# A post-norm layer on one core: short contractions filled up to 128 rows, and two sums of Wo on another engine

## The chip, the core and the metric

The kernel runs on one core of a Trainium2 chip. A core has five engines that run their own instruction streams and wait for one another through semaphores: TensorE (PE in the profile; its weight loads are listed apart as PEld), VectorE (DVE), ScalarE (ACT), GpSimd (POOL), and SyncE (SP), which here only issues DMAs. The metric is the device time of one execution in microseconds. All arithmetic is in 32-bit floats; each matmul of the program appears in the trace as two PE instructions, each transpose on PE as one.

## The reference

One layer: attention with rotary positions and a causal mask, then a layer norm, then a dense layer with a routed low-rank addition, then a layer norm.

```python
x = layernorm(x + attention(x, Wq, bq, Wk, bk, Wv, bv, Wo, bo))
x = layernorm(x + ffn(x, ...))

def ffn(x, W_base, b_base, lora_A, lora_B, router_W, router_b, domain_prior, active):
    y = einsum('bth,oh->bto', x, W_base) + b_base
    z = einsum('bth,erh->bter', x, lora_A[active])
    contribs = einsum('bter,eor->bteo', z, lora_B[active]) * 2.0
    logits = (einsum('bth,eh->bte', x, router_W) + router_b)[..., active]
    alpha = softmax(log(domain_prior[active] + 1e-12) + logits)
    return y + einsum('bteo,bte->bto', contribs, alpha)
```

x is (2, 512, 512): 2 sequences of 512 tokens with 512 features. There are 32 query heads and 8 key heads of 128; 4 of 16 experts are active, each with 8 low-rank rows, so A has 32 rows (EAR) and the router 4 (EA).

## The kernel before

The attention is worked in 16 units (a key head and a sequence each). A unit has 16 slots; a slot is one block of 32 tokens by 4 query heads, 128 rows of scores. The function `slot(T)` writes out by hand, for every slot T, what each engine is given: on PE a score matmul, pieces of the next unit's query projection, of the key and value projections, of the output projection of an earlier unit, and the product of the probabilities with v; on DVE the masked maximum of slot T-1, the reciprocals of T-2, the 32x32 transposes of T-4, the rotations of q and k and the adds into x_sb; on ACT the exponentials and the copies. The score has two PSUM banks, so a score needs the exponential of two slots earlier to be done. Engines work strictly in the order written. Work that isn't tied to each slot is put at a slot with `put(T, f)` and is given out at that slot's end.

The projections use a scheme of seven instead of eight block products, which needs sums and differences of blocks beforehand. For the output projection these are the four of `wo_sums` (L621): step 0 makes t1 = b12 - b11, step 1 makes t2 = b22 - t1, step 2 overwrites b12 with b22 - b12, step 3 makes t4 = b21 - t2, each over 128x512 elements. `wo_products` (L638) reads t2 in its step 2 and t1 in its step 3, two and three slots after the set of weights comes in, b12 in step 4 and t4 in step 6. A set serves both sequences of a key head, except for the last two key heads, which are worked one sequence at a time ("single"). For the single sets the four sums stand on POOL, one slot before the set comes in (L930); only two single sets take this path, since the last two sets use the plain product `wo_mm`. POOL also makes the sums of the context (`ctx_sums`, L633), of Wq (`w_sums`, L426), and the last addition of each rotation (L376).

In the setup, the rows of A and of the router are gathered into ar_act (36 partitions) and transposed on PE into arT (L284, tile ta); B is transposed into the first 32 rows of bmT, whose row 32 is the bias b_base (33 partitions); the prior, replicated over 128 columns in lp_rep (4 partitions), is spread over the partitions by a product with the identity (L312, tile pl).

After the attention each of the 8 token tiles is an object `Ffn`. `base` multiplies the normed tile with W_base, A and the router (L767); `logits` and `alphas` make the weighted factor zs on DVE and ACT; `low_rank` transposes it on PE (L803, tile tz) and copies it on DVE into the first 32 rows of zT, whose row 32 is ones (L743, 33 partitions); `finish` (L808) adds zT times bmT, two matmuls of 256 columns; `add` adds the residual and starts the second norm's statistics (L814, L693). The last tile, fc, takes its base product in two halves with the same low-rank product at their end (L829), and `route` (L771) for A and the router. The order of these calls is written out by hand at the end of the kernel (L1089 to L1203), partly between the last slots.

Of the kernel before, what the change touches and what calls it, by code (L numbers as in the profile page):

```python
# [9 lines left out]
F32 = mybir.dt.float32  # L10
I32 = mybir.dt.int32
AF = mybir.ActivationFunctionType
ALU = mybir.AluOpType
AX = mybir.AxisListType

P = 128
# [13 lines left out]
def postln_layer_kernel(  # L30
# [33 lines left out]
    nc = tc.nc  # L64
    B, S, HID = x.shape
# [4 lines left out]
    O = W_base.shape[0]  # L70
    OC = O // P
    EA = active.shape[0]
    EAR = EA * RK
# [19 lines left out]
    def set_of(u):  # L93
        return u // B if u < MIXED else MIXED // B + u - MIXED

    def set_units(n):
        return [u for u in range(NU) if set_of(u) == n]
# [4 lines left out]
    const = ctx.enter_context(tc.tile_pool(name="const", bufs=1))  # L102
# [18 lines left out]
    OH, ARH = O // 2, EAR // 2  # L121
    WX_COLS = OH + ARH + EA
    arT = const.tile([P, KC, EAR + EA], F32, name="arT")
    bmT = const.tile([EAR + 1, O], F32, name="bmT")
    lp_bc = const.tile([P, EA], F32, name="lp_bc")
    ident = const.tile([P, P], F32, name="ident")
    maskw = const.tile([P, S], F32, name="maskw")
# [14 lines left out]
    setup = setup_stack.enter_context(tc.tile_pool(name="setup", bufs=1))  # L142
# [41 lines left out]
    for r in range(QB):  # L184
        nc.gpsimd.tensor_copy(maskw[ts(r, BLK), S - BLK :], tri[ts(r, BLK), r, :])
    nc.gpsimd.memset(eps_sb, LN_EPS)
    for z in zt:
        nc.gpsimd.memset(z, 0.0)

# [28 lines left out]
    nc.gpsimd.dma_start(out=act_p, in_=active.partition_broadcast(P))  # L218
    lane = setup.tile([P, 1], I32, name="lane")
    nc.gpsimd.iota(lane, pattern=[[0, 1]], base=0, channel_multiplier=1)  # L220
    ar_act = setup.tile([EAR + EA, HID], F32, name="ar_act")
    rb_act = setup.tile([EA, 1], F32, name="rb_act")
    pr_act = setup.tile([EA, 1], F32, name="pr_act")
    b_act = setup.tile([P, EA, BJ * RK], F32, name="b_act")
# [1 line left out]
    idx = {}  # L226
# [31 lines left out]
    def gather(dst, src, rows):  # L258
        nc.gpsimd.indirect_dma_start(
            out=dst, out_offset=None, in_=src,  # L260
            in_offset=bass.IndirectOffsetOnAxis(ap=rows, axis=0),
        )

    def gather_experts():
        gather(ar_act[:EAR, :], lora_A.rearrange("e r n -> (e r) n"), idx["a"])
        gather(ar_act[EAR:, :], router_W, idx["e"])
        for a in range(EA):
            gather(b_act[:, a, :], lora_B.rearrange("e (p j) r -> (e p) (j r)", j=BJ), idx["b"][:, a : a + 1])

# [10 lines left out]
    def lora_weights(step):  # L280
        if step == 0:
            ta = ps_wo.tile([P, KC, EAR + EA], F32, tag="wx", name="ta")
            for c in range(KC):
                nc.tensor.transpose(ta[:, c, :], ar_act[:, ts(c, P)], ident[: EAR + EA, : EAR + EA])  # L284
            nc.vector.tensor_copy(arT, ta)
            nc.vector.tensor_copy(b_jar, b_act.rearrange("p a (j r) -> p j a r", r=RK))
        else:

            tbm = ps_wo.tile([EAR, BJ, P], F32, tag="wx", name="tbm")
            for j in range(BJ):  # L290
                nc.tensor.transpose(tbm[:, j, :], b_jar[:, j, :, :].rearrange("p a r -> p (a r)"), ident)
            nc.vector.tensor_copy(bmT[:EAR, :].rearrange("k (p j) -> k j p", j=BJ), tbm)

    pr = {}

    def prior_weights(step):

        if step == 0:
            pr_eps = setup.tile([EA, 1], F32, name="pr_eps")
            nc.vector.tensor_scalar(pr_eps, pr_act, PRIOR_EPS, None, ALU.add)  # L300
            pr["lp"] = setup.tile([EA, 1], F32, name="lp")
            nc.scalar.activation(pr["lp"], pr_eps, AF.Ln)
        elif step == 1:
            lpb = setup.tile([EA, 1], F32, name="lpb")
            nc.vector.tensor_tensor(lpb, pr["lp"], rb_act, ALU.add)
            ones = setup.tile([EA, P], F32, name="ones")
            nc.vector.memset(ones, 1.0)
            pr["rep"] = setup.tile([EA, P], F32, name="lp_rep")
            nc.vector.tensor_scalar(pr["rep"], ones, lpb, None, ALU.mult)
        else:  # L310
            pl = ps_wo.tile([P, EA], F32, tag="wx", name="pl")
            nc.tensor.matmul(pl, lhsT=pr["rep"], rhs=ident[:EA, :EA], start=True, stop=True)  # L312
            nc.vector.tensor_copy(lp_bc, pl)


# [302 lines left out]
    def wo_block(n, c_half, n_half):  # L618
        return wos[n][:, CH * c_half : CH * (c_half + 1), ts(n_half, NHALF)]

    def wo_sums(n, step, engine=nc.vector):  # L621

        if step == 0:
            wt[n] = wow.tile([P, 3, CH, NHALF], F32, tag="wt", name=f"wt_{n}", bufs=1)
        t1, t2, t4 = (wt[n][:, m] for m in range(3))
        b11, b12, b21, b22 = (wo_block(n, c_half, n_half) for c_half in range(2) for n_half in range(2))
        engine.tensor_tensor(
            *((t1, b12, b11), (t2, b22, t1), (b12, b22, b12), (t4, b21, t2))[step], ALU.subtract)
# [54 lines left out]
    class Norm:  # L683


        def __init__(self, pool, n, name):
            self.mv = pool.tile([P, n, 2], F32, name=f"mv_{name}")
            self.rstd = pool.tile([P, n], F32, name=f"rstd_{name}")
            self.pool = pool
# [43 lines left out]
    class Ffn:  # L733
# [3 lines left out]
        def __init__(self, t, banks, norm1, norm2, i):  # L737
            self.t, self.banks, self.norm1, self.norm2, self.i = t, banks, norm1, norm2, i
            self.x = x_sb[:, t, :]
            self.xT = ffn_pool.tile([P, KC, P], F32, name=f"x1T_{t}")  # L740
            self.y = ffn_pool.tile([P, O], F32, name=f"y_{t}")

            self.zT = ffn_pool.tile([EAR + 1, P], F32, name=f"zT_{t}")  # L743
            nc.gpsimd.memset(self.zT[EAR:, :], 1.0)

        def own(self, shape, name):
            return ffn_pool.tile(shape, F32, name=f"{name}_{self.t}")
# [113 lines left out]
    def put(slot, f):  # L861
        extra.setdefault(slot, []).append(f)
# [3 lines left out]
    def v_tile(gg, t, pool, tag):  # L866
        for c in range(KC):
            v_mm(gg, t, c, pool, tag)

    put(T_BEGIN, gather_experts)  # L870
    for n, gg, t in [(2 * t - 1, 0, TPB + t) for t in range(TPB)] + [(2 * t + 11, 1, t) for t in range(TPB)]:
        put(n, lambda gg=gg, t=t: v_tile(gg, t, ps_wo, "wx"))
# [4 lines left out]
    for k in range(3):  # L877
        put(-4 + k, lambda k=k: prior_weights(k))
        if k < 2:
            put(12 + 4 * k, lambda k=k: lora_weights(k))  # L880
# [41 lines left out]
    def wo_from(u):  # L922
        return UNIT * u + LAG_WO
# [3 lines left out]
    for n in range(NSETS - 2):  # L927
        single = len(set_units(n)) == 1
        for k in range(4):
            put(wo_from(set_units(n)[0]) + (-1 if single else (0, 1, 1, 3)[k]),  # L930
                lambda n=n, k=k, engine=nc.gpsimd if single else nc.vector: wo_sums(n, k, engine))


    weigh_at = {}
# [137 lines left out]
    ffn_pool = ctx.enter_context(tc.tile_pool(name="ffn", bufs=1))  # L1072
# [181 lines left out]
```

## Time and profile before

| | us |
|---|---|
| median of 3 runs (lowest to highest) | 826.52 (826.05 to 826.85) |
| the profiled execution | 826.17 |
| its span, first to last instruction | 824.2 |
| PE busy in the span | 814.9 |
| DVE busy | 598.2 |
| POOL busy | 327.8 |
| PE granted clock | 0.999 |

The profiled execution took 1.97 us more than its span; what is worked out from the trace is a difference of spans. Lines of the profile name an engine, a line of the kernel, the operation, the tiles written and read, the partitions and elements, and the count; times are in microseconds from the start of the span. A matmul's form such as 33*128 33x256 is weights of 33 rows and 128 columns and moving data of 33 rows and 256 columns. Matmuls overlap, so durations of neighbours add up to more than the time between their starts.

### The profile page before, as it was taken

The page shows a single profiled execution, that of the slowest core. Times are in us where ns is not written, and L with a number is a line of the kernel's source. Part 1 is how long each engine was busy: PE and PEld are TensorE (multiplying, and loading weights), DVE is VectorE, ACT ScalarE, POOL GpSimd, SP SyncE. Part 2 cuts the span into 40 slices and gives each one's busy share as a digit, 9 for nine tenths or more (in the row PEclk, how much of TensorE's full clock was granted, in tenths as well). Part 3 has the DMA queues.
Part 4 walks back from the last instruction along what each step waited for, and adds up shares of the span by engine and source line. Part 5 has one row for each costly group of instructions (what it writes and reads, how often), then busy time and mean ns, then how long its engine had stood idle before and what let it go on. Part 6 is the DMA issues. An engine that isn't in the chain of part 4 may idle for free.

```text
span 824.2 us, 11178 instructions
## 1 busy us (share of the span) xinstructions
PE 814.9 (99%) x3381; PEld 596.9 (72%) x3381; DVE 598.2 (73%) x1964; ACT 379.0 (46%) x1058; POOL 327.8 (40%) x374
## 2 busy tenths in 40 slices
PE   9999999999999999999999999999999999999997
PEld 5567777777777778777777878777777777655565
DVE  5368877687879886787867786787867678973445
ACT  1236453553545454545535454445535454563254
POOL 6464343511534445322443245353445626410032
PEclk9999999999999999999999999999999999999999
DMA  9015627445465636364554536365544636474211
GB/s 293 34 50 150 203 73 194 126 121 160 117 177 137 183 90 206 89 159 148 149 146 115 179 90 205 91 187 170 137 136 121 195 84 202 138 254 142 77 38 64
DMA packets 84414, 115.99 MB, mean 141 GB/s; under 512 B 6525, under 2 KB 64237, under 8 KB 82306
## 3 DMA queue, kind: packets, MB, share of 16 engines
q1 hardware_dynamic: 83682, 114.98, 48.3%
q8 instruction: 27, 0.44, 0.2%
q0 software_dynamic: 448, 0.14, 0.2%
q14 instruction: 33, 0.27, 0.1%
q10 hardware_dynamic: 224, 0.16, 0.1%
HBM read 71.21 MB, written 44.04 MB: 140 GB/s over the span
## 4 chain that ended last, share of the span: by engine, by line
PE 94%; DVE 2%; POOL 2%; DMA 1%; ACT 0%; issue 0%; SPq 0%; DVEq 0%; POOLq 0%
PE pc L602 16%; PE sc L546 14%; PE qx L434 11%; PE wx L434 11%; PE qy L434 9%; PE wy L434 8%; PE pp L355 5%; PE kx L434 4%; PE vx L512 4%; PE py L767 3%; PE po L674 3%; PE pv L338 3%; PE tp L275 1%; PE py L808 1%; DMA pT<-db 1%; DMA db<-zt 0%
## 5 line engine op out<-in xcount | busy, mean ns | idle before, releaser
L554 DVE CUSTOM_DVE_ANT_0 sc<-sc,maskw 128x288 f32<-128x288 f32 (+15 forms) x256 | 114.2, 446 | 146.3 <-PE sc L546 144.7
L561 ACT ACTIVATE p<-sc,nmax 128x288 f32<-128x288 f32 (+15 forms) x256 | 124.3, 485 | 202.8 <-DVE nmax L554 180.4
L602 PE MATMUL pc<-pT,v 128*128 128x512 f32 x320 | 165.5, 599 | 0.1
L546 PE MATMUL sc<-kT,qT 128*128 128x160 f32 (+15 forms) x512 | 162.0, 398 | 0.2 <-ACT p L561 0.2
L376 POOL TENSOR_TENSOR qT<-q,t 128x512 f32<-128x512 f32 x56 | 76.5, 1366 | 171.4 <-DVE q L375 171.4
L569 ACT ACTIVATE p<-p,den 128x288 f32<-128x288 f32 (+15 forms) x256 | 133.2, 521 | 0.0
L546 PEld LDWEIGHTS sc<-kT,qT 128*128 128x128 f32 x512 | 95.9, 190 | 23.5 <-issue 9.3
L609 ACT ACTIVATE ctxT<-pc,bqkT 128x512 f32<-128x512 f32 x64 | 44.0, 688 | 117.5 <-PE pc L602 117.5
L421 POOL TENSOR_TENSOR cs<-ctxT 128x256 f32<-128x256 f32 x28 | 22.2, 793 | 157.8 <-PE wy L434 93.7
L577 DVE STREAM_TRANSPOSE zt<-p 128x128 f32<-128x128 f32 (+2 forms) x192 | 81.6, 425 | 0.0
L602 PEld LDWEIGHTS pc<-pT,v 128*128 128x128 f32 x320 | 57.0, 190 | 19.2 <-issue 5.7
L470 ACT COPY q<-qx 128x256 f32<-128x256 f32 x112 | 41.4, 369 | 36.5 <-PE qx L434 36.5
L434 PE MATMUL qx<-xs,wq 128*128 128x256 f32 x224 | 58.0, 381 | 0.0
L434 PE MATMUL wx<-wo,ctxT 128*128 128x256 f32 x224 | 57.6, 379 | 0.0
L434 PEld LDWEIGHTS qx<-xs,wq 128*128 128x128 f32 x224 | 41.4, 190 | 22.3 <-issue 18.4
L579 DVE STREAM_TRANSPOSE zt<-p 128x32 f32<-128x32 f32 (+3 forms) x256 | 57.5, 224 | 0.0
L561 ACT ACTIVATION_READ_ACCUMULATOR p<-sc,nmax 128x1 f32 x256 | 49.8, 195 | 0.0
L434 PEld LDWEIGHTS wx<-wo,ctxT 128*128 128x128 f32 x224 | 42.5, 190 | 7.7 <-issue 1.2
L368 DVE SCALAR_TENSOR_TENSOR t<-q,bqkT,rope_sb 64x512 f32<-64x512 f32 x56 | 45.9, 820 | 1.5
L660 DVE TENSOR_TENSOR x_sb<-wx,x_sb 128x256 f32<-128x256 f32 x112 | 47.0, 420 | 0.0
L371 DVE SCALAR_TENSOR_TENSOR t<-q,bqkT,rope_sb 64x512 f32<-64x512 f32 x56 | 43.4, 775 | 1.3
L565 DVE RECIPROCAL den<-den 128x1 f32<-128x1 f32 x256 | 39.3, 153 | 1.5 <-ACT p L561 1.2
(224 smaller groups left out, 1481.9 us busy)
## 6 DMA issues: line engine op xcount, KB each, us to landing
db<-zt SPq DMA_DIRECT2D x64, 256.0 KB, 3.9
pT<-db SPq DMA_DIRECT2D x16, 1024.0 KB, 4.8
db<-zt SPq DMA_DIRECT2D x64, 192.0 KB, 3.3
pT<-db SPq DMA_DIRECT2D x16, 768.0 KB, 4.3
wq<-in_L_attn_Wq_dram SPq DMA_DIRECT2D x20, 512.0 KB, 5.4
wo<-in_L_attn_Wo_dram SPq DMA_DIRECT2D x10, 1024.0 KB, 8.0
db<-zt SPq DMA_DIRECT2D x64, 128.0 KB, 2.4
pT<-db SPq DMA_DIRECT2D x16, 512.0 KB, 4.1
```

The lines of the kernel that those rows point to most:

```text
L368: nc.vector.scalar_tensor_tensor(t2[lo, :], q[hi, :], b_ap[hi, :], rope_sb[hi, 1, :], ALU.add, ALU.mult)
L376: nc.gpsimd.tensor_tensor(dst, t1[:, :].rearrange("p (n s) -> p n s", s=BLK), t2[:, :].rearrange("p (n s) -> p n s", s=BLK), ALU.add)
L434: nc.tensor.matmul(ps, lhsT=wt[:, c, :], rhs=xt[:, c, :], start=start and c == 0, stop=c == CH - 1, skip_group_check=True)
L546: nc.tensor.matmul(sc[s][:, :w], lhsT=qT[u][:, i * QB + n].rearrange("p r s -> p (r s)"), rhs=kT[u][:].rearrange("p n s -> p (n s)")[:, :w ...
L554: nc.vector.tensor_tensor_reduce(sc[s][:, :w], sc[s][:, :w], maskw[:, S - w :], -SCALE, -MASKED, ALU.add, ALU.min, nmax[s])
L561: nc.scalar.activation(ptile[s][:, :w], sc[s][:, :w], AF.Exp, bias=nmax[s], scale=-1.0, accum_out=rden[s])
L569: nc.scalar.activation(ptile[s][:, :w], ptile[s][:, :w], AF.Copy, scale=rden[s])
L577: nc.vector.transpose(z[:, :, last - i : last, n, :].rearrange("p q j s -> p j q s"), ptile[s][:, : i * P])
L579: nc.vector.transpose(z[:, : n + 1, last, n, :], ptile[s][:, i * P : w])
L602: nc.tensor.matmul(psc[p], lhsT=v_sb[g // VG, b][:, j, ts(g % VG, D)], rhs=pT[p][:, :, ts(j, P)], start=(j == 0), stop=(j == i))
L609: nc.scalar.activation(ctxT[p], psc[p], AF.Identity, bias=bqkT[:, col : col + 1])
L660: nc.vector.tensor_tensor(into, pw[k, bank], into, ALU.add)
```

## The change

Four tiles get 128 partitions instead of 33, 36 or 4 and are filled with zeros by POOL: bmT and zT (the low-rank product), ar_act (the rows of A and the router) and lp_rep (the prior). The matmuls that read them take all 128 partitions. The transposes of ar_act become products with the first 36 columns of the identity. Apart from that, of the four sums of a single set's Wo, steps 0 and 1 go to DVE, step 0 in the slot where it was and step 1 one slot later, and steps 2 and 3 stay on POOL, one slot later.

```diff
-    bmT = const.tile([EAR + 1, O], F32, name="bmT")
+    bmT = const.tile([P, O], F32, name="bmT")
...
     nc.gpsimd.memset(eps_sb, LN_EPS)
+    nc.gpsimd.memset(bmT, 0.0)
     for z in zt:
         nc.gpsimd.memset(z, 0.0)
...
-    ar_act = setup.tile([EAR + EA, HID], F32, name="ar_act")
+    ar_act = setup.tile([P, HID], F32, name="ar_act")
+    lp_rep = setup.tile([P, P], F32, name="lp_rep")
+    for part in (ar_act, lp_rep):
+        nc.gpsimd.memset(part, 0.0)
...
-        gather(ar_act[EAR:, :], router_W, idx["e"])
+        gather(ar_act[EAR : EAR + EA, :], router_W, idx["e"])
...
-                nc.tensor.transpose(ta[:, c, :], ar_act[:, ts(c, P)], ident[: EAR + EA, : EAR + EA])
+                nc.tensor.matmul(
+                    ta[:, c, :], lhsT=ar_act[:, ts(c, P)], rhs=ident[:, : EAR + EA], start=True, stop=True)
...
-            pr["rep"] = setup.tile([EA, P], F32, name="lp_rep")
-            nc.vector.tensor_scalar(pr["rep"], ones, lpb, None, ALU.mult)
+            nc.vector.tensor_scalar(lp_rep[:EA, :], ones, lpb, None, ALU.mult)
...
-            nc.tensor.matmul(pl, lhsT=pr["rep"], rhs=ident[:EA, :EA], start=True, stop=True)
+            nc.tensor.matmul(pl, lhsT=lp_rep, rhs=ident[:, :EA], start=True, stop=True)
...
-            self.zT = ffn_pool.tile([EAR + 1, P], F32, name=f"zT_{t}")
-            nc.gpsimd.memset(self.zT[EAR:, :], 1.0)
+            self.zT = ffn_pool.tile([P, P], F32, name=f"zT_{t}")
+            nc.gpsimd.memset(self.zT, 0.0)
+            nc.gpsimd.memset(self.zT[EAR : EAR + 1, :], 1.0)
...
-            put(wo_from(set_units(n)[0]) + (-1 if single else (0, 1, 1, 3)[k]),
-                lambda n=n, k=k, engine=nc.gpsimd if single else nc.vector: wo_sums(n, k, engine))
+            put(wo_from(set_units(n)[0]) + ((-1, 0, 0, 0) if single else (0, 1, 1, 3))[k],
+                lambda n=n, k=k, engine=nc.gpsimd if single and k > 1 else nc.vector: wo_sums(n, k, engine))
```

## The prediction

> **What bounds the kernel now.** I read the busy times first, then the waits of the TensorE (PE), then the chain that ended last, then PE and its weight loads (PEld) in order of time in the stretches where the diff acts, and at last VectorE (DVE) and GpSimd (POOL) there. The page's head and the whole answer on PE's waits:
>
> ```profile
> span 824.2 us, 11178 instructions
> PE 814.9 (99%) x3381; PEld 596.9 (72%) x3381; DVE 598.2 (73%) x1964; ACT 379.0 (46%) x1058; POOL 327.8 (40%) x374
> ...
> PE 94%; DVE 2%; POOL 2%; DMA 1%; ACT 0%; issue 0%; SPq 0%; DVEq 0%; POOLq 0%
> ...
> PE wx L434 <- POOL wt L627: 1.3, 1, 1.3
> PE idle L1036 <- DVE maskw L175: 1.2, 1, 1.2
> PE pp L355 <- ACT xT L276: 0.5, 1, 0.5
> PE tp L275 <- ACT xT L276: 0.2, 1, 0.2
> PE sc L546 <- ACT p L561: 0.2, 1, 0.2
> ```
>
> PE is the bound: of 824.2 us it is idle some 9, half of that after its last matmul. Only what shortens PE's own stream, or a wait of PE, can move the time. Outside the start there is one real wait, 1.3 us for a sum of Wo on POOL (L627). PE and POOL in order of time there (start, duration, engine, line; the bracket is the idle time before):
>
> ```profile
> 695.01 1.02 PE L602 MATMUL pc<-pT,v 128*128 128x512 f32 x2
> 697.35 1.13 PE L434 MATMUL wx<-wt,cs 128*128 128x256 f32 x4 [1.31 <-POOL wt L627]
> ...
> 693.01 1.26 POOL L376 TENSOR_TENSOR qT<-q,t 128x512 f32<-128x512 f32 x1
> 694.24 1.72 POOL L627 TENSOR_TENSOR wt<-wo 128x512 f32<-128x512 f32 x1
> 696.03 1.26 POOL L627 TENSOR_TENSOR wt<-wo,wt 128x512 f32<-128x512 f32 x1
> ```
>
> Two 128x512 matmuls take 0.86 us everywhere else, so PE was free at 695.87 and started at 697.35: 1.48 us lost. The product needs the second sum, which POOL ends at 697.29.
>
> The second thing is not shown as a wait. PE and, below it, PEld around the low-rank product (L808, 33 rows):
>
> ```profile
> 757.40 1.02 PE L602 MATMUL pc<-pT,v 128*128 128x512 f32 x2
> 758.36 1.13 PE L808 MATMUL py<-bmT,zT 33*128 33x256 f32 x4
> 759.41 0.70 PE L546 MATMUL sc<-kT,qT 128*128 128x256 f32 x2
> 759.95 1.88 PE L674 MATMUL po<-wo,ctxT 128*128 128x512 f32 x4
> ...
> 757.22 0.38 PEld L602 LDWEIGHTS pc<-pT,v 128*128 128x128 f32 x2
> 758.35 0.73 PEld L808 LDWEIGHTS py<-bmT,zT 33*128 33x128 f32 x4 [0.76 <-issue]
> 759.41 0.30 PEld L546 LDWEIGHTS sc<-kT,qT 128*128 128x128 f32 x2 [0.33 <-ACT ctxT L609]
> ```
>
> Starts are to be subtracted, not durations. The pair before takes 0.96 us to the next start (0.86 elsewhere), the four of 256 columns 1.05 (0.87 for qx, qy, wx and wy, 128 rows), the score after them 0.54 (0.43 for the same shape at 698.32). So 0.10 on entering, 0.18 inside, 0.11 on leaving: 0.39 us for one group. PEld says why: other weights are loaded 0.2 us ahead of their matmul (757.22 for a matmul at 757.40), those of the 33-row group, and the first 128-row ones after it, only as the matmul starts.
>
> **What the Trainium skill says.** "TensorEngine Tiling (Array Packing)", Key Properties: changing the tiling mode drains TensorE; 64-row and 32-row modes are listed beside the 128-row one. "TensorE: Matmul & The Clock Gate", Step-by-step: weights are pulled ahead of running matmuls only where the row groups don't conflict or the background buffer is meant. The trace agrees as far as it goes: every group with 33, 36 or 4 rows shows the excess, and the transpose tz (L803: 128 rows, 32 columns) shows none (755.20 to 755.30, the neighbour before it 0.86), so it is the rows and not the small shape. "SBUF — State Buffer", Who interferes with whom: a DVE instruction with two SBUF inputs and a GpSimd one that reads SBUF shut each other out, GpSimd writes alone do not. The trace agrees: L627 on DVE takes 0.65 to 0.69 us alone and up to 1.38, its wo form up to 1.75, beside a POOL sum.
>
> **Part 1, padding.** The same excess, start minus start minus the 128-row rate, at the nine groups of the end: 0.39 (758.36), 0.38 (774.41), 0.38 (780.34), 0.35 (799.12), 0.30 (805.38), 0.39 (810.55), 0.32 (L829, 813.97), 0.37 (815.67), 0.21 (the last): 3.1 us of PE. With 128 rows I expect all of it gone, as 128-row groups of this size show none. Not all reaches the end, because other engines become late next:
> - At 778.41 tz waits for zs on DVE, behind the adds of the group at 774.41. Those start on that group's first half, which comes 0.2 earlier, not 0.38: 0.18 is lost.
> - From 805.49 DVE and ACT work without a gap (logits, exp, table load, adds, statistics) until zT at 809.98 and the next logits at 810.94; tz at 810.35 already follows zT by 0.1 us. So the 0.30 at 805.38 gains nothing, and what the groups at 810.55 and 813.97 gain is spent waiting for DVE: DVE's own wait for ph (0.25) and for the group at 815.67 can shrink by about 0.5 together, and the last chain (y, statistics, root, y, store) starts from there.
> So 0.39 + 0.20 + 0.38 + 0.35 before 805, and 0.5 after: 1.8 us. Bounds: 0 (the excess has another cause) and 3.1.
>
> In the setup, ta (L284, 36 rows) takes 0.37 with 0.19 around it; as a plain matmul it has 8 instructions instead of 4, and zl (L775, the same shape, 128 rows) takes 0.82: 0.26 worse. pl (L312, 4 rows) loses some 0.1 of its margins. Net 0.15 worse, on PE's path. The memsets are all on POOL. bmT's (0.47 us at the zt rate, 1.37 for 1536 columns) lies before the index loads, so act_p lands at 15.4 instead of 14.9; DVE reads it at 15.36, and behind it the q rotations have 1.6 us before PE wants the bank, and 2.88 of idle time later. Without that cover it would cost at most 0.5. ar_act and lp_rep (0.6) fall into POOL's 4.75 us idle at 9.4. bmT's row load on SP is issued at 10.59, long after the memset. Eight zT memsets (0.15 to 0.2 each, 1.5) lie in POOL's 3.7 us idle before 718.4. Nothing for all these.
>
> **Part 2, Wo's sums.** Only two sets (at 647 and 694) have the form touched; on DVE's and POOL's order four sums change engine and nothing else moves, PE's and SP's orders are unchanged. At 647 PE doesn't wait: 0. At 694 the first sum goes behind L375 (ends 689.63), the second behind L371 of kT (ends 692.4). Each costs 0.65 to 0.69, up to 1.4 if POOL's cs sums hold the inputs. I place the second's end at about 695, before 695.87, so the 1.48 goes. Then DVE is late next: queued behind the sums are the masked maxima, whose exponentials free the score banks. DVE has 0.39 + 1.10 idle here (both waiting for PE), gets 1.34 of work, and is full from 698.95 to 711.40. POOL has 2.5 us less, and the waits that POOL put into DVE's L371, L375, L368, L371 (1.28, 1.48, 1.25, 1.87 against 0.71 to 0.75, 3 us) should partly go. Walking slot by slot I find one score (352 wide) waiting 0.3 and the rest following PE. Value 1.3; bounds -1 (every sum and rotation locked) and 1.5.
>
> **Sum.** 1.8 + 1.3 - 0.15 = 2.95 us. The profiled execution took 826.17 (span 824.2 and 1.97 around it): 823.2. The median of the runs is 826.52, 0.35 above; on that scale 823.5.
>
> **Rivals.**
> - A, all of PE's savings reach the end: 3.1 + 1.4 - 0.15 = 4.35, 822.2. For it: PE shows next to no waits. Against: DVE's gapless stretch after 805.49.
> - B, the padding changes nothing (the excess comes from the wait for zT, or the array switches anyway): 1.3 - 0.3 = 1.0, 825.5. For it: zT comes from DVE just before. Against: tz waits for DVE as well and shows no excess, and the excess lies on the leaving side too.
> - C, VectorE takes over from POOL at 694: the stall shrinks by 0.3 only. 1.8 + 0.3 - 0.15 = 1.95, 824.6. For it: DVE is full right after.
> - D, slower: POOL locks DVE out. Place 689 to 704; price 1.75 for each sum and 1.1 for each of two kT rotations, 5.7 us in all. It decides the sign once DVE's addition exceeds its idle 1.49, the 1.48 of stall and the 1.7 of Part 1 less setup, 4.7: then 1.0 slower, 827.5. Against: POOL has two sums less.
>
> **How the numbers follow.** Forecast 0.52, A 0.20, B 0.12, C 0.12, D 0.04. About 0.2% (1.65 us, under 824.87) is what can be told from no change. Faster: forecast, A and most of C, less the forecast's weak tail, 0.80; the same: B and the rest, 0.15; slower 0.05. The range goes from A with the whole 1.5 and the runs' scatter (821.8) to B (825.6), which leaves D and the edges out.
>
> **What would show it.** Right: L808 at 128 rows, start to next start 0.87, PEld ahead of it; no wait of PE on wt; tz near 778 and 810 waiting for DVE. Wrong: L808 still at 1.05 (B); a new wait of PE's scores for exponentials between 696 and 712 (C, D); or PE savings of 3 us and a tail after PE's last matmul no longer than 5.3 us (A).

## The result and the profile after

| | before | after |
|---|---|---|
| median, us | 826.38 (12 runs) | 824.45 (12 runs) |
| span of the profiled execution, us | 824.2 | 822.4 |
| PE busy, us | 814.9 | 812.3 |

The ratio is 0.9978 with a 95% interval of 0.997 to 0.9986: 1.9 us faster. The forecast was 823.5, one microsecond less; its range (821.8 to 825.6) holds the result. The number is nearest to that of rival C (824.6).

The page of the kernel after, its head, its chain, and the answer on what PE waited for (total, times, longest):

```profile
span 822.4 us, 11201 instructions
PE 812.3 (99%) x3385; PEld 598.2 (73%) x3385; DVE 600.6 (73%) x1968; ACT 379.3 (46%) x1058; POOL 326.7 (40%) x381
...
PE 92%; DVE 5%; ACT 1%; POOL 1%; issue 1%; DMA 1%; SPq 0%; DVEq 0%; POOLq 0%
...
PE wx L440 <- DVE den L571: 0.7, 1, 0.7
...
PE tz L810 <- DVE zs L801: 0.3, 1, 0.3
PE py L815 <- DVE zT L811: 0.2, 1, 0.2
```

Line numbers have moved by 6 or 7 (L434 is L440, L808 is L815, L627 is L633). The wait on POOL's wt is gone. In its place stands one for DVE, and DVE's share of the chain is 5% where it was 2%. PE is 2.6 us less busy, but the span is only 1.8 shorter.

Where the time came and went is read best by pairing the same score matmul in both traces and subtracting the start times. The difference changes at a few places only:

```
place in the trace of after            after - before there, us
 45   the start                        +0.07
 73   behind ta (36 rows -> 128)       +0.41
697.3 behind the wx that waited        -1.07
698.9                                  -0.71
702.0                                  +0.19
705.8                                  +0.09
755   before the first product         +0.04
816   PE's last matmuls                -2.04
822   the end of the span              -1.8
```

So there are three accounts. The setup costs 0.34 at ta (before it, pl gives 0.08, and a load of x_sb at the start came 0.15 later). The stall of 1.48 us goes, and 1.16 of it is lost again by 706. The low-rank product gives 1.84 up to the end of the span: 1.32 up to tz at 804.37, which starts at 803.09, and 0.52 behind it. First the low-rank product, PE and its weight loads in order of time (start, duration, line):

```profile
757.45 1.02 PE L608 MATMUL pc<-pT,v 128*128 128x512 f32 x2
758.31 1.03 PE L815 MATMUL py<-bmT,zT 128*128 128x256 f32 x4
759.17 0.59 PE L552 MATMUL sc<-kT,qT 128*128 128x256 f32 x2
759.60 1.88 PE L680 MATMUL po<-wo,ctxT 128*128 128x512 f32 x4
...
757.88 0.19 PEld L815 LDWEIGHTS py<-bmT,zT 128*128 128x128 f32 x1 [0.24 <-issue]
```

From start to start it is now 0.86, 0.86 and 0.43, where it was 0.96, 1.05 and 0.54: the 0.39 us of one group are gone on all three sides. The first weights are loaded at 757.88, 0.43 before their matmul; before, they were loaded as it started.

Then the place of the stall. PE, DVE's instructions that matter, and one of POOL, each in order of time:

```profile
696.31 1.10 PE L440 MATMUL wx<-wt,cs 128*128 128x256 f32 x4
697.25 0.59 PE L552 MATMUL sc<-kT,qT 128*128 128x256 f32 x2
697.93 1.13 PE L440 MATMUL wy<-wt,cs 128*128 128x256 f32 x4
...
699.39 1.02 PE L608 MATMUL pc<-pT,v 128*128 128x512 f32 x2
701.08 1.10 PE L440 MATMUL wx<-wo,ctxT 128*128 128x256 f32 x4 [0.67 <-DVE den L571]
...
690.04 1.22 DVE L633 TENSOR_TENSOR wt<-wo 128x512 f32<-128x512 f32 x1
...
693.90 1.65 DVE L633 TENSOR_TENSOR wt<-wo,wt 128x512 f32<-128x512 f32 x1
...
697.47 0.41 DVE L666 TENSOR_TENSOR x_sb<-wy,x_sb 128x256 f32<-128x256 f32 x1
...
698.52 1.61 DVE L374 SCALAR_TENSOR_TENSOR t<-q,bqkT,rope_sb 64x512 f32<-64x512 f32 x1
700.16 0.43 DVE L560 CUSTOM_DVE_ANT_0 sc<-sc,maskw 128x256 f32<-128x256 f32 x1
...
700.51 0.42 DVE L666 TENSOR_TENSOR x_sb<-wx,x_sb 128x256 f32<-128x256 f32 x1
...
701.32 0.74 DVE L377 SCALAR_TENSOR_TENSOR t<-q,bqkT,rope_sb 64x512 f32<-64x512 f32 x1
...
698.32 1.27 POOL L382 TENSOR_TENSOR kT<-kT,t 128x512 f32<-128x512 f32 x1
```

The kernel before, the same two rotations with the add between them, and the product of step 4:

```profile
696.59 1.25 DVE L368 SCALAR_TENSOR_TENSOR t<-q,bqkT,rope_sb 64x512 f32<-64x512 f32 x1
...
699.30 0.42 DVE L660 TENSOR_TENSOR x_sb<-wx,x_sb 128x256 f32<-128x256 f32 x1
...
700.10 1.87 DVE L371 SCALAR_TENSOR_TENSOR t<-q,bqkT,rope_sb 64x512 f32<-64x512 f32 x1
...
700.95 1.03 PE L434 MATMUL wx<-wo,ctxT 128*128 128x256 f32 x4
```

The wx product starts at 696.31, 0.03 after PE is free (695.42 and 0.86): the sum of Wo is no longer late. But two later products are. wy at 697.93 could have started at 697.68, and wx at 701.08 at 700.25: 0.25 and 0.83 late, which together with weights that were not loaded ahead gives the 1.16 of the table (within 0.1). What they read has long been there (the last of it is b12 for wx, which POOL ends at 696.69); what they lack is their PSUM bank. In `wo_products` and `wo_adds` the bank wx is accumulated in step 2, read by DVE's add into x_sb in step 3, and accumulated further in step 4, so step 4 has to wait for the add. Bank wy is read in step 2 and written anew in step 3. That add ends at 700.93, and the wy add at 697.88, each just before the product. The view names "den L571", the instruction behind the add on DVE, as the releaser; `den` has nothing to do with wx. The trace also holds PE's own instruction that waits for DVE's semaphore there, which the timeline leaves out: it goes through 0.04 us after the add has ended and 0.03 before `den` has, and the same in the kernels with the sums alone and with POOL's spread below. So it is the add.

### The profile page after: what moved, and what is told of

It is laid out like the page before. It is cut to its first block, busy times and chain, and to the rows that moved or that the text cites. A ratio compares the mean times of both kernels' runs of the same rounds, so it can differ in the third digit from the quotient of the medians.

```text
span 822.4 us, 11201 instructions
## 1 busy us (share of the span) xinstructions
PE 812.3 (99%) x3385; PEld 598.2 (73%) x3385; DVE 600.6 (73%) x1968; ACT 379.3 (46%) x1058; POOL 326.7 (40%) x381
## 4 chain that ended last, share of the span: by engine, by line
PE 92%; DVE 5%; ACT 1%; POOL 1%; issue 1%; DMA 1%; SPq 0%; DVEq 0%; POOLq 0%
PE pc L608 16%; PE sc L552 14%; PE qx L440 11%; PE wx L440 11%; PE qy L440 9%; PE wy L440 8%; PE pp L361 5%; PE kx L440 4%; PE vx L518 4%; PE po L680 3%; PE py L774 3%; PE pv L344 3%; PE tp L281 1%; DMA x_sb<-_attn_hidden_states_dram 1%; DVE sc L560 1%
## 5 line engine op out<-in xcount | busy, mean ns | idle before, releaser
L440 PE MATMUL wx<-wo,ctxT 128*128 128x256 f32 x224 | 57.7, 380 | 0.7 <-DVE den L571 0.7
L440 PE MATMUL qx<-xs,wq 128*128 128x256 f32 x224 | 58.0, 381 | 0.0
L440 PEld LDWEIGHTS qx<-xs,wq 128*128 128x128 f32 x224 | 41.4, 190 | 22.2 <-issue 18.4
L440 PEld LDWEIGHTS wx<-wo,ctxT 128*128 128x128 f32 x224 | 42.4, 190 | 8.7 <-issue 2.2
L374 DVE SCALAR_TENSOR_TENSOR t<-q,bqkT,rope_sb 64x512 f32<-64x512 f32 x56 | 46.3, 827 | 1.5
L377 DVE SCALAR_TENSOR_TENSOR t<-q,bqkT,rope_sb 64x512 f32<-64x512 f32 x56 | 42.5, 759 | 1.3
L571 DVE RECIPROCAL den<-den 128x1 f32<-128x1 f32 x256 | 39.3, 153 | 1.4 <-ACT p L567 1.2
```

The source lines that it names most:

```text
L374: nc.vector.scalar_tensor_tensor(t2[lo, :], q[hi, :], b_ap[hi, :], rope_sb[hi, 1, :], ALU.add, ALU.mult)
L440: nc.tensor.matmul(ps, lhsT=wt[:, c, :], rhs=xt[:, c, :], start=start and c == 0, stop=c == CH - 1, skip_group_check=True)
```

## The experiments

Four kernels that take the change apart come first: the padding alone, the sums alone, the product alone padded to 128 rows, and to 64.

**The padding alone, the sums alone.** The changed kernel with the old placing of the sums, and the kernel before with the new one:

```diff
 # in the changed kernel, for the padding alone; the other way round in the kernel before
-            put(wo_from(set_units(n)[0]) + ((-1, 0, 0, 0) if single else (0, 1, 1, 3))[k],
-                lambda n=n, k=k, engine=nc.gpsimd if single and k > 1 else nc.vector: wo_sums(n, k, engine))
+            put(wo_from(set_units(n)[0]) + (-1 if single else (0, 1, 1, 3)[k]),
+                lambda n=n, k=k, engine=nc.gpsimd if single else nc.vector: wo_sums(n, k, engine))
```

> The four tiles padded as in the changed kernel, Wo's sums as before. If padding carries nearly all of the gain (1.84 us at the end, less 0.27 lost in the setup's ta and pl): 1.6 us under the kernel before, some 824.8, the product L815 at 0.86 to 0.87 us from start to next start, and the wait of PE for wt on POOL back at 1.3 us. If the moved sums carry a good part of it, as the prediction had it (1.3 of 2.95): less than 1 us under it, over 825.4.

> Only Wo's sums moved, nothing padded. If DVE takes over from POOL: 0.3 us under the kernel before, some 826.1, PE's wait on wt gone but a wait of about 0.7 for an add of DVE near 700. If the stall is really removed: 1.3 us under it, 825.1.

The padding alone: 824.77 against 826.33, ratio 0.9978 (0.9969 to 0.9987). The sums alone: 825.7, ratio 0.9998 (0.999 to 1.0006), no change that can be told; the median lies between the two forecasts, and the trace decides. With the padding alone the wait on POOL's wt is back at 1.3 us. With the sums alone the score matmuls are 1.39 us ahead of the kernel before at 698, 0.11 at 701.8 and 0.23 at 705.7: the same loss as in the changed kernel, without any padding. (Another 0.34 comes at 725, where the kernel before waits for a load of pT; the kernel with the product alone, which leaves the sums where they were, shows the same 0.34, so it isn't the sums'.) PE's wait for the add:

```profile
700.77 1.10 PE L434 MATMUL wx<-wo,ctxT 128*128 128x256 f32 x4 [0.68 <-DVE den L565]
```

So most of the change's gain, 1.6 of 1.9 us by the medians, is the padding's, and the loss in Part 2 does not come from the padding.

**The product alone, with 128, 64 and 96 rows.** Only bmT and zT are filled up; ta and pl stay as they were.

```diff
-    bmT = const.tile([EAR + 1, O], F32, name="bmT")
+    bmT = const.tile([P, O], F32, name="bmT")     # 64 and 96 in the other two
...
+    nc.gpsimd.memset(bmT, 0.0)
...
-            self.zT = ffn_pool.tile([EAR + 1, P], F32, name=f"zT_{t}")
-            nc.gpsimd.memset(self.zT[EAR:, :], 1.0)
+            self.zT = ffn_pool.tile([P, P], F32, name=f"zT_{t}")
+            nc.gpsimd.memset(self.zT, 0.0)
+            nc.gpsimd.memset(self.zT[EAR : EAR + 1, :], 1.0)
```

> Only the low-rank product padded (zT and bmT at 128 partitions); ta, pl and Wo's sums as before. If the end's gain is all the product's: 1.8 us under the kernel before, 824.55, and faster than the kernel with all four tiles padded by 0.27. If padding ta and pl helps too: not faster than that one.

> As the run with the low-rank product at 128 partitions, but zT and bmT at 64. If the excess comes from leaving the 128-row mode of the array: no gain, 826.4, L808's four matmuls at 1.05 us from start to next start and their weights loaded only as they start. If it falls with the number of rows, a third of it goes: 825.8. If any multiple of 32 will do: 824.55.

> The low-rank product at 96 partitions. If the array has no mode between 64 and 128 rows, so that 96 rows run in the 128-row mode: the whole gain, 1.9 us under the kernel before, some 824.4, the product's four matmuls at 0.86 to 0.87 us from start to next start. If only the full 128 rows are free of the excess: 826.3 and 1.05 us.

| rows | median, us | ratio (95%) | start to next start of the group |
|---|---|---|---|
| 128 | 824.4 | 0.9981 (0.9971 to 0.999) | 0.86 |
| 96 | 824.56 | 0.9977 (0.9968 to 0.9987) | 0.87 |
| 64 | 826.32 | 1.0004 (0.9993 to 1.0016) | 1.06 |

The first group with 64 rows, and with 96:

```profile
758.47 1.13 PE L810 MATMUL py<-bmT,zT 64*128 64x256 f32 x4
759.53 0.70 PE L547 MATMUL sc<-kT,qT 128*128 128x256 f32 x2
```

```profile
758.38 1.03 PE L810 MATMUL py<-bmT,zT 96*128 96x256 f32 x4
759.25 0.60 PE L547 MATMUL sc<-kT,qT 128*128 128x256 f32 x2
```

Filling up to 64 rows gains nothing, to 96 everything. This shows that the rows given to the matmul set the price: the zeros, the memsets and the wait for zT are the same in all three. It fits what the Trainium skill says in "TensorEngine Tiling (Array Packing)", Available Configurations and Key Properties: a mode of 64 rows beside that of 128, and a drain when the mode changes. No run shows the modes themselves; that 96 rows cost what 128 do is what these runs add. The product alone was also 0.37 us faster than all padding together (824.4 against 824.77), on the side that ta's 0.34 in the trace gives, though a difference so small lies within the runs' scatter.

**Where the sums stand.** If DVE's queue is what takes the stall's gain back, the sums should be free where DVE has room. These kernels have the product padded and all four sums six to three slots earlier than in the kernel before, which the set's weights allow as they land much earlier; t1, t2 and t4 of the first of these sets get a buffer of their own for it. In one all four are on POOL, in the other the first two are on DVE, as in the change. A third leaves DVE's two where the change has them and spreads POOL's.

```diff
-            wt[n] = wow.tile([P, 3, CH, NHALF], F32, tag="wt", name=f"wt_{n}", bufs=1)
+            wt[n] = (late["pool"] if n == NSETS - 4 else wow).tile(
+                [P, 3, CH, NHALF], F32, tag="wt", name=f"wt_{n}", bufs=1)
...
-            put(wo_from(set_units(n)[0]) + (-1 if single else (0, 1, 1, 3)[k]),
-                lambda n=n, k=k, engine=nc.gpsimd if single else nc.vector: wo_sums(n, k, engine))
+            put(wo_from(set_units(n)[0]) + ((-7, -6, -5, -4) if single else (0, 1, 1, 3))[k],
+                lambda n=n, k=k, engine=nc.gpsimd if single and k > 1 else nc.vector: wo_sums(n, k, engine))
...
 # all on POOL: engine=nc.gpsimd if single else nc.vector
 # POOL's spread: the old buffer, and (-1, 0, 1, 3) for (-7, -6, -5, -4)
```

> The product at 128 partitions, and all four sums of a single set on POOL as in the kernel before, but 3 to 6 slots earlier, where POOL is idle; the first single set's sums get a tile of their own. If DVE's load and its collisions with POOL took back the stall's gain: the stall of 1.3 to 1.5 goes and is not given back, about 1.3 us under the run with the product alone, some 823.1. If DVE bounds this stretch in any case once PE doesn't wait: at most 0.4 under it, 824.0.

> As the run with the four sums early on POOL, but the first two of them on DVE, at the same early slots, so DVE has the same 1.3 us of added work as in the changed kernel, only elsewhere. If place and collisions matter: near the run with all four early on POOL, 823.1 to 823.4. If DVE's amount of work matters: 824.0, like the changed kernel's sums.

> The product at 128 partitions, the first two sums on DVE at the changed kernel's slots, but POOL's two sums one and three slots later. If the give-back comes from POOL's sums and its rotation of k standing before DVE's rotation at L369 (1.61 us instead of 0.75): that one runs at 0.75, PE's wait of 0.7 for the add of wx shrinks, and 0.6 to 0.9 more of the stall's gain stays, 823.5 against 824.1. If DVE's two sums alone are what it can't carry: 824.1, no better.

All on POOL and early: 822.75, ratio 0.9959 (0.9944 to 0.9973). Two on DVE and early: 822.66, ratio 0.9961 (0.9948 to 0.9974). POOL's spread: 824.25, ratio 0.9974 (0.9965 to 0.9983), no better than the change. DVE and then PE of the kernel with the early sums on DVE:

```profile
673.27 0.68 DVE L629 TENSOR_TENSOR wt<-wo 128x512 f32<-128x512 f32 x1
677.25 0.69 DVE L629 TENSOR_TENSOR wt<-wo,wt 128x512 f32<-128x512 f32 x1
...
696.80 0.75 DVE L369 SCALAR_TENSOR_TENSOR t<-q,bqkT,rope_sb 64x512 f32<-64x512 f32 x1
...
698.72 1.02 PE L603 MATMUL pc<-pT,v 128*128 128x512 f32 x2
699.58 1.03 PE L435 MATMUL wx<-wo,ctxT 128*128 128x256 f32 x4
```

The two sums that took 1.22 and 1.65 take 0.68 and 0.69, the rotation (L374 of the changed kernel) 0.75 instead of 1.61, and wx follows the product before it by 0.86. The engine makes no difference that can be told here (822.75 and 822.66); the place does: 1.7 us under the kernel with the product alone, of which the trace shows the whole stall gone (1.58) and none of it lost again. The intervals of these ratios and of the product's just overlap, so this rests on the trace as much as on the medians. In the profile with all sums on POOL, PE waits once 0.85 us near 724, for a DMA of pT, away from the sums.

The spread kernel is a miss. POOL's sums were to leave the rotation alone, and did not. The rotation and POOL's instructions around it:

```profile
698.48 1.84 DVE L369 SCALAR_TENSOR_TENSOR t<-q,bqkT,rope_sb 64x512 f32<-64x512 f32 x1
...
697.28 1.27 POOL L377 TENSOR_TENSOR kT<-kT,t 128x512 f32<-128x512 f32 x1 [2.12 <-DVE kT L376]
698.51 1.27 POOL L628 TENSOR_TENSOR wo<-wo 128x512 f32<-128x512 f32 x1
```

Here the moved sum ran against the rotation from 698.51 on; in the changed kernel it was POOL's addition for kT, at 698.32 with the two sums ahead of it (695.25 with the early sums). Only the partner of the collision changed, and PE's wait was 0.90 us.

**Half of the sums left out.** From the kernel with the padded product and the change's sums, in one POOL's two sums of the single sets are left out (t4 is set to zero, b12 stays as it is), in the other DVE's two (t1 and t2 are set to zero by POOL).

```diff
 # POOL's left out
+        if len(set_units(n)) == 1 and step > 1:
+            if step == 3:
+                nc.gpsimd.memset(t4, 0.0)
+            return
 # DVE's left out
+        if len(set_units(n)) == 1 and step < 2:
+            nc.gpsimd.memset((t1, t2)[step], 0.0)
+            return
```

> The product at 128 partitions and the changed kernel's sums, but POOL's two sums of the single sets left out (b12 keeps its value, t4 is set to zero by a memset of POOL, which reads nothing), so the output is another one. DVE's two sums stay where the changed kernel has them. If the give-back comes from POOL's sums holding DVE up at L369 and L381: L369 near 698.3 takes 0.75 and not 1.6, PE waits at most 0.3 near 700, and some 0.9 of the stall's gain stays: 823.3. If DVE's two sums there are too much by themselves: PE's wait of 0.7 stays, 824.1.

> The reverse: DVE's two sums of the single sets left out (t1 and t2 are set to zero by memsets of POOL), POOL's two where the changed kernel has them; the output is another one. If either half of the pair is enough to take the gain back: near 824. If DVE's sums, held up by POOL's sums of the context and its rotation, are what makes DVE late: PE follows without a wait and 1.3 stays, 823.0.

Without POOL's sums: 823.05, ratio 0.9961 (0.9946 to 0.9977). Without DVE's: 822.98, ratio 0.9961 (0.9949 to 0.9973). In neither does PE wait at the wx of step 4. DVE in the first, then in the second kernel:

```profile
693.88 1.65 DVE L632 TENSOR_TENSOR wt<-wo,wt 128x512 f32<-128x512 f32 x1
...
699.45 0.42 DVE L665 TENSOR_TENSOR x_sb<-wx,x_sb 128x256 f32<-128x256 f32 x1
```

```profile
696.87 1.62 DVE L369 SCALAR_TENSOR_TENSOR t<-q,bqkT,rope_sb 64x512 f32<-64x512 f32 x1
...
698.88 0.42 DVE L664 TENSOR_TENSOR x_sb<-wx,x_sb 128x256 f32<-128x256 f32 x1
```

Each keeps one half of the trouble. Without POOL's sums, DVE's second still takes 1.65, beside POOL's addition for qT and not beside POOL's sums; but the rotation (0.75) comes free, and the add out of wx ends at 699.87, 1.06 earlier than in the changed kernel. Without DVE's, the rotation still takes 1.62, but starts 1.65 earlier, and the add ends at 699.30. The changed kernel needed it by 700.25 and had it at 700.93, 0.68 late: either 1.06 or 1.63 is enough (PE's own starts differ by up to 0.14 here), and in both kernels the add is done before PE is free for wx, which starts at 700.04 and 699.65. So neither half alone takes the gain back (0.17 of it without POOL's sums, nothing without DVE's); it needs DVE's two sums and POOL's two behind them.

**What is lost at the end.** Part 1's forecast had PE wait for zs near 778, where logits and weights stand on DVE behind the adds of the tile before, and again in the last 20 us. On top of the early sums, one kernel puts the logits and weights of the third tile ahead of those adds; the next reorders the end as well, so that no low-rank product stands right behind its own factor.

```diff
+    put(A + 15, lambda f=f0[2]: (f.logits(), f.alphas()))
     for f, at in zip(f0, (A + 5, A + 11, A + 13)):
...
-        put(at + 2, lambda f=f: (f.logits(), f.alphas()))
+        if f is not f0[2]:
+            put(at + 2, lambda f=f: (f.logits(), f.alphas()))
...
 # the second kernel besides
     fa[0].finish()
-    fa[0].add()
-    fa[0].norm2.sqrt(0, 1)
     for c in range(KC):
         fb.base(c)
-        if c == 2:
+        if c == 1:
             fa[1].low_rank()
+    fa[0].add()
     fc.low_rank()
-    fa[0].norm2.invert(0, 1)
-    fa[0].store()
     fb.logits()
     fb.alphas()
+    fa[0].norm2.sqrt(0, 1)
     fa[1].finish()
     fa[1].add()
+    fa[0].norm2.invert(0, 1)
+    fa[0].store()
...
+    fb.low_rank()
     fc.half_end(0)
...
-    fb.low_rank()
     for c in range(KC):
```

> The run with the first two sums early on DVE, and the logits and weights of the third tile given out before the adds of the second, in the same slot. If tz near 778 waits for zs only because DVE does these adds first (0.46 us of PE): PE's wait there goes and 0.3 to 0.5 of it reaches the end, 822.2. If DVE's gapless stretch after 805 takes it: the wait goes and the time stays at 822.6.

> As before, and in the last 17 us the transposes and copies of zT given out before the adds and statistics that DVE now does first, and a root moved behind the exponential, so that ScalarE loads one table less in between. If the last 1.3 us of the padding's PE savings are lost to DVE's and ACT's chain there: PE's waits for zT near 809 and 814 shrink and 0.5 to 1.0 more reaches the end, 821.5. If the tail after PE's last matmul takes it, because the adds now come later: 822.2, with PE's end earlier and a longer tail.

The first: 822.08, ratio 0.9951 (0.9937 to 0.9964). The second: 821.8, ratio 0.9947 (0.9934 to 0.9961). Both are faster than the kernel before and than the change (their intervals lie below its 0.997 to 0.9986). Their lowest and highest runs overlap (821.56 to 822.52, and 820.91 to 823.61), so which of the two is better is not settled by the medians; the same holds for the first against the early sums on DVE (822.15 to 825.97). PE of the first where zs was late:

```profile
774.58 1.02 PE L603 MATMUL pc<-pT,v 128*128 128x512 f32 x2
775.44 0.27 PE L806 MATMUL tz<-ident,zs 128*32 128x128 f32 x1
775.55 1.88 PE L676 MATMUL po<-wo,ctxT 128*128 128x512 f32 x4
```

tz follows by 0.86; the 0.3 us wait is gone. The second kernel's profile began 2.25 us late, at the first load of x_sb, ahead of all that differs. Its list of waits no longer has the product's for zT, but one of 0.3 us for another zs:

```profile
806.90 0.28 PE L806 MATMUL tz<-ident,zs 128*32 128x128 f32 x1 [0.27 <-DVE zs L797]
807.03 2.01 PE L770 MATMUL py<-wbT,x1T 128*128 128x272 f32 x8
```

Because the start differs from profile to profile, spans are set side by side without it (the span less the offset to the kernel before at 45 us): before 824.2, after 822.3, product alone 822.1, early sums on DVE 820.5, early logits 820.1, reordered end 819.6. Single executions each; the order is that of the medians. In the second PE ends 0.5 earlier than in the first, and the tail behind PE's last matmul is as long (5.6 in both), so in this one execution the whole 0.5 reaches the end.

## Why the prediction was right or wrong

- **The cause in Part 1: right.** The excess of 33-row groups was to be the row mode, and rival B said it wasn't. 64 rows leave all of it, 96 rows nothing.
- **The size of Part 1: right.** 3.1 us of PE were to give 1.8 at the end; from 755 to the end of the span the trace shows 1.84, and its two parts fit as well (1.32 and 0.5 forecast, 1.32 and 0.52 found). The losses are where the forecast put them: tz at 777.87 starts 0.46 behind the matmuls ahead of it, where it was 0.27, so 0.19 is lost (0.18 forecast; the list of waits has 0.30 of it), and the product at 813.93 waits for zT, 0.21 by the list. In between, tz at 809.00 starts 0.24 behind the matmuls ahead of it, which the list of waits doesn't show. After PE's last matmul the span goes on for 5.6 us, 5.3 before: what PE gained in the last groups was spent on DVE's side. Rival A needed a tail no longer than 5.3.
- **The setup: right.** ta costs 0.34 (0.26 forecast: of the 0.19 around it only the half ahead of it went, and the group behind it still takes 0.95), pl gives 0.08 (0.1). The memsets cost nothing that the traces show.
- **Part 2: the mis-sized term.** 1.3 forecast, 0.32 in the trace (1.48 less 1.16). The stall went as forecast; the failed step is the walk through DVE's slots behind it. It took the two sums at 1.34 in all, their price alone, and they took 2.87, because POOL's context sums and its addition for qT were running; the bound named in the same place (up to 1.4 each) was nearer. It counted on the waits that POOL puts into DVE's rotations to shrink with two sums fewer on POOL. In sum they did, the four it names took 4.41 for 5.88, but 1.13 of that is the last one's (L377, 0.74 for 1.87), which stands behind the add out of wx. Ahead of that add they took 3.67 for 4.01, and the nearest of them, L374, grew to 1.61 (L368, its counterpart before, 1.25): POOL's addition for kT came at 698.32 and no longer at 700.16, so it met this rotation and not the one behind the add. And it looked for the next late thing in the score banks, where the exponentials are awaited, though the add out of the wx bank stands in the same queue and PE needs it between two accumulations. Nothing in the profile before showed a wait for this add, but its margin could have been worked out: in the trace before, the add ends at 699.72 and the product of step 4 starts at 700.95, 1.23 later. The stall's end takes 1.48 from that, DVE's idle time gives at most 1.49, and the sums take 1.34 even at the forecast's price: 0.1 short. The rotations ahead of the add gave 0.34, and the sums took 1.53 above that price.
- **Rival C** had the number, 824.6 against 824.45, and the mechanism in outline: DVE in POOL's place. It had been given 0.12; "DVE is full right after" was said for it and not followed up. The sign named for it, PE's scores waiting for exponentials between 696 and 712, did not come either (PE's list has 0.2 us of it, at 722 and as before): neither the forecast nor a rival named the add. Rival D (DVE slowed until the kernel is slower) was nearest on the sums' collisions (2.87 found, 3.5 in its price), but not on the two rotations of kT, which took 2.06 for 2.76 before; the price stayed under the 4.7 us from which it would have decided.
- **The sum.** 1.84 + 0.32 - 0.26 = 1.90 from the traces, against 2.95: of the 1.05 missing, 0.98 is Part 2. The result lies inside the range because that reached from A to B, not because this term was right.

The Trainium skill's "SBUF — State Buffer", Who interferes with whom, which the prediction cited, is borne out more strongly than it was used: from 688 to 706 every DVE duration that grew is of an instruction with two inputs from SBUF beside a POOL addition, and the adds that read PSUM kept their 0.41 to 0.42.

## What to carry to other kernels

A matmul with few rows of contraction, alone in a stream of 128-row ones, is to be judged by start minus start of its neighbours too, since no wait shows its price; filling it up with zeros to 96 or 128 rows took it away here, to 64 it didn't. When work is moved off an engine that is late, first ask whether it can be done earlier: with a buffer of its own the same work three to six slots earlier cost PE nothing that the traces show, on either engine, while on the other engine at nearly the same place it lost 1.16 of the 1.48 us that it had gained. When walking an engine's queue for what is late next, include the reads of accumulators between two accumulations, and price every instruction beside what the engine with the shared inputs is doing at that moment.

## What was not expected of the hardware

- 96 rows cost as little as 128 (0.87 and 0.86 us for the group), and 64 as much as 33 (1.06 and 1.05).
- The plain product in place of a 36-row transpose (ta) went from 0.37 to 0.81 us from start to next start: more rows, but twice the instructions.
- A rotation on 64 partitions (64x512, two inputs from SBUF) took 0.75 us alone and 1.15 to 1.87 beside POOL's additions, and POOL's addition of 128x512 up to 1.72 instead of 1.27.
- With 128 rows everywhere a group of four 256-column matmuls still took 0.95 us and not 0.86 right behind eight narrow ones (36 columns): behind ta at 72.20 and behind zl at 804.01. Its weights came only 0.03 ahead there, behind the eight loads of the narrow ones; that this is the reason was not tested.
